# Layer 2 of a four-layer kernel: the third tile is fetched one step earlier, and the second step's order is rewritten

## The chip, the cores and the metric

The kernel runs on one core of one Trainium2 chip. The metric is the device time of one execution in microseconds (us), given as the median of three runs. All stages run one after the other in one launch, so a microsecond saved anywhere on the path is a microsecond of the total.

## The reference

Four layers work on the same array `x` of 32 x 64 x 512 floats, 2048 rows of 512. Each adds a feed-forward part to `x`: an attention and mixture-of-experts block (layer 0), a mixture of 32 experts (layer 1), a soft mixture of experts behind a low-rank adapter (layer 2), and an attention over cached blocks with an int8 product (layer 3). The change lies in layer 2:

```python
H = einsum('btd,od->bto', x, W)
delta = einsum('btr,bor->bto', einsum('btd,brd->btr', x, A[idx]), Bm[idx]) * s[idx]
y = H + delta                                  # the adapter product
x_ln = layernorm(y); x_n = l2norm(x_ln)
logits = einsum('bnd,des->bnes', x_n, mu_n)    # 16 experts x 128 slots = 2048 slots
dispatch = softmax(logits, over the 64 rows n of one batch entry)
combine = softmax(logits, over the 2048 slots of one row)
h = gelu(einsum('besd,edh->besh', einsum('bnd,bnes->besd', x_ln, dispatch), W1) + b1)
out = einsum('bsd,bns->bnd', h @ W2 + b2, combine)
x = x + out
```

## The kernel before

**Tiles and steps.** The 2048 rows are 16 tiles of 128 rows (two batch entries each). `layer2` has a loop over `i` from 0 to 16, here called step 0, step 1 and so on. Step `i` computes the logits and both softmaxes of tile `i` (class `Softmaxes`), mixes tile `i-1` (class `Mix`), and forms the adapter product and norm of tile `i+1` (class `Lora` and `l2_norm_pieces`). Tiles 0 and 1 are fetched and put through the adapter ahead of the loop.

**Pieces of a step.** `logits(q)` (L1396, four quarters of 512 slots) writes `lp`; VectorE scales it into `lT` (L1401) and keeps a running maximum `mx` (L1409 to L1413). `over_rows(q)` is the first softmax (`eT`: L1421, L1422, the Exp at L1425), and `divide(q)` divides by its sums (`inv` on VectorE at L1432 and L1433, the product on GpSimd at L1434). `highest()` transposes `mx` (PE L1440), takes the row maximum (`mr`, L1442) and spreads it on a diagonal (`dg`, L1444). `over_slots()` multiplies that diagonal by ones (`bp`, PE L1450), subtracts it from the four `lT` (VectorE L1452) and takes their Exp (ScalarE L1453). `hidden(q)` is the product with W1 (`zp`, PE L1473; `z`, VectorE L1475). `turn(q)` transposes weights (`ep` L1482, copied to `ew` L1484), `sums()` adds the slots' weights (`csum` L1492, `csb` L1497), `dispatch(q)` is the product `hp` (L1505) with its Gelu (`h`, L1510), `total()` is the product `dp` (L1515) with its reciprocal `rd`, `combine(q)` the product `gp` (L1528) with its copy `gT`, `project(q)` the product `out` (L1539). `Lora.turn`, `.adapter` and `.product` are the PE products `tp` (L1320, copied to `fT` on ScalarE at L1322), `ap` (L1329, masked into `am` at L1333) and `yp` (L1341, L1342). `l2_norm_pieces` begins with the statistics `st`, `mv`, `ve` (L1360 to L1364).

**Fetching a tile.** `combined.fetch` loads a tile's rows (`xt`), gathers four rows of expert outputs for each row (`yk`, GpSimd's queue, L284), and hands back four additions (VectorE L1025) which the step places by hand. Before the change tile 2 is fetched in step 1, tile 3 in step 2, and so on.

**`hidden` moves between steps.** In step 0 there is nothing to mix, so step 0 computes `hidden` of tile 0 itself. Step 1 therefore has no `hidden` pieces. From step 2 on, each step computes the four `hidden` pieces of the tile that it mixes, and puts them beside `highest` and `over_slots`.

**Order.** [...] `g.pin` and `g.first` fix instructions in the order in which the program writes them. `cache_rows` is a side job: each `next(rows)` gathers 112 rows on GpSimd's queue (`kvst`, one buffer) and writes them back by SP's queue (`oldkv`). It lies in the same GpSimd queue as the gathers of `fetch` and the products of `divide`. PSUM has two buffers under the tag `tp`, which `tp`, `ap`, `bp`, `ep` and `dp` share, and two under `mm`, which `lp`, `zp`, `csum` and `yp` share.

Of the kernel before, what the change touches and what calls it, by code (L numbers as in the profile page):

```python
# [22 lines left out]
NT = B * T // P  # L23
# [1155 lines left out]
def layer2(g, w, combined, first, w3):  # L1179
    tc, nc, a = g.tc, g.nc, g.a  # L1180
    with ExitStack() as ctx:
        pool = lambda name, bufs, **kw: ctx.enter_context(
            tc.tile_pool(name=name, bufs=bufs, reuse_waits="tile", **kw)
        )
        wp = pool("l2w", 1)
        sb = pool("l2sb", 1)
        s2 = pool("l2s2", 2)
        ps = pool("l2ps", 2, space=PSUM)
        xs, xb = g.stream("x2"), g.stream("x2b")
        x = [combined(sb, 0, 3), combined(sb, 1, 3)]  # L1190
        for k in ("gamma", "beta"):
            w[k] = g.load_bcast(wp, k)
        yp = [Lora(g, w, sb, s2, ps, x[i], i).run() for i in range(2)]
        xn = l2_norm(g, w, sb, s2, yp[0])
        w["b1"] = g.load_bcast(wp, "b1", eng=nc.scalar, later=True)
        for k in ("w2", "b2"):
            w[k] = g.load(wp, k, nc.scalar, True)
        w["bias3"] = g.load_bcast(wp, "bias3", eng=nc.scalar, later=True)
        xnT, nn = g.transpose4(ps, s2, xn[0], "xnT2"), xn[1]
        xn = l2_norm(g, w, sb, s2, yp[1])  # L1200


        last = None
        rows = cache_rows(g, sb, w3)
        for i in range(NT + 1):
            soft = Softmaxes(g, w, sb, s2, ps, xnT) if i < NT else None
            mix = Mix(g, w, sb, s2, ps, x[i - 1], *last) if last else None
            adds = []
            if last and i + 1 < NT:
                t, adds = combined.fetch(sb, i + 1, 3)  # L1210
                x.append(t)
            if mix and not soft:
                mix.turn(0)
                mix.turn(1)
            if soft:
                for q in range(4):
                    soft.logits(q)
                    if mix and q < 2:
                        mix.turn(q)
                    soft.over_rows(q)  # L1220
                    if q % 2 == 0:
                        next(rows, None)
                    if q > 0:
                        soft.divide(q - 1)
            if i == 0:
                z = Mix(g, w, sb, s2, ps, None, None, None, xnT, nn, None)
            else:
                z = mix if mix.z is None else None
            if z:
                z.hidden(0)  # L1230
            if soft:
                soft.divide(3)
            for add in adds[0:2]:
                add()
            if z:
                z.hidden(1)
                next(rows, None)
            if soft:
                soft.highest()
            for add in adds[2:4]:  # L1240
                add()
            if z:
                z.hidden(2)
            if soft:
                soft.over_slots()
            if z:
                z.hidden(3)
                next(rows, None)
            if mix:
                lora = Lora(g, w, sb, s2, ps, x[i + 1], i + 1) if i + 1 < NT else None  # L1250
                if lora:
                    lora.turn()
                mix.sums()
                mix.dispatch(0)
                if lora:
                    lora.adapter()
                mix.turn(2)
                if lora:
                    norm = l2_norm_pieces(g, w, sb, s2, lora.product())
                    next(norm)  # L1260
                    if i + 2 == NT:

                        w3["w_kv3"] = first.tile([P, 4, D], F32, name="w_kv3", tag="sb_w_2")
                        g.dma(w3["w_kv3"], a["w_kv3"])
                        w3["x3"] = [first.tile([P, D], F32, name="x3", tag=f"sb_{k}") for k in ("w_a", "w_b")]
                        for j in range(2):
                            g.dma(w3["x3"][j], xs[j * P : (j + 1) * P, :])
                mix.total()
                mix.combine(0)
                mix.dispatch(1)  # L1270
                mix.turn(3)
                if lora:
                    next(norm)
                mix.project(0)
                next(rows, None)
                mix.combine(1)
                if lora:
                    xn = next(norm)
                mix.dispatch(2)
                mix.project(1)  # L1280
                mix.combine(2)
                mix.dispatch(3)
                mix.project(2)
                next(rows, None)
                mix.combine(3)
            before = xnT, nn
            if i + 1 < NT:
                xnT, nn = g.transpose4(ps, s2, xn[0], "xnT2", pin=True), xn[1]
            if mix:
                mix.bias()  # L1290
                mix.project(3)
                mix.finish(xs, xb, i - 1)
            last = (soft.eT, soft.lT, *before, z.z if i == 0 else None) if soft else None
        for _ in rows:
            pass
        return xs, xb


def cache_rows(g, sb, w3):

    w3["rows"] = g.dram.tile([B, 3, CH, D], F32, name="oldkv")
    for b in range(B):
        for c in range(3):
            t = sb.tile([CH, D], F32, name="kvst", bufs=1)
            g.gather(t, g.a["kv"], w3["gidx"][0:CH, c * B + b : c * B + b + 1], later=True)
            g.dma(w3["rows"][b, c], t)
            yield
# [43 lines left out]
def l2_norm(g, w, sb, s2, yp):  # L1351

    *_, out = l2_norm_pieces(g, w, sb, s2, yp)
    return out


def l2_norm_pieces(g, w, sb, s2, yp):
    nc = g.nc
    st = s2.tile([P, 6], F32, name="st")
    g.pin(nc.vector.bn_stats(st, yp))  # L1360
    mv = s2.tile([P, 2], F32, name="mv")
    nc.vector.bn_aggr(mv, st)
    ve = s2.tile([P, 1], F32, name="ve")
    g.pin(nc.vector.tensor_scalar(ve, mv[:, 1:2], 1e-5, None, ALU.add))  # L1364
    rs = g.power(s2, ve, "nhalf", "rs")
    yield
    xl = sb.tile([P, D], F32, name="xl")
    g.pin(nc.vector.tensor_scalar(xl, yp, mv[:, 0:1], rs, ALU.subtract, ALU.mult))
    nc.gpsimd.tensor_tensor(xl, xl, w["gamma"], ALU.mult)
    nc.gpsimd.tensor_tensor(xl, xl, w["beta"], ALU.add)  # L1370
    sq = sb.tile([P, D], F32, name="sq2", tag="mx")
    ss = s2.tile([P, 1], F32, name="ss2")
    nc.scalar.activation(sq, xl, AF.Square, accum_out=ss)
    nn = g.power(s2, ss, "half", "nn")
    yield
    g.pin(nc.vector.tensor_scalar(nn, nn, 1e-12, None, ALU.max))  # L1376
    rn = s2.tile([P, 1], F32, name="rn")
    nc.vector.reciprocal(rn, nn)
    g.pin(nc.vector.tensor_scalar(xl, xl, rn, None, ALU.mult))
    yield xl, nn  # L1380
# [749 lines left out]
def program(tc, a):  # L2130
    with ExitStack() as ctx:
        g = Prog(tc, a, ctx)
        w3 = {}
        pool3 = ctx.enter_context(tc.tile_pool(name="w3", bufs=1))
        bridge, combined = layer0(g, w3, pool3)
        first = ctx.enter_context(tc.tile_pool(name="w2a", bufs=1, reuse_waits="tile"))
        with tc.tile_pool(name="w2", bufs=1, reuse_waits="tile") as pool:
            w2 = {"pool": pool}
            beside = layer2_ahead(g, first, pool, w2)
            combined = layer1(g, bridge, combined, beside, w2)  # L2140
            for _ in beside:
                pass
            xs, xb = layer2(g, w2, combined, first, w3)
        layer3(g, w3, xs, xb)
# [17 lines left out]
```

## Time and profile before

| | us |
|---|---|
| median of 3 runs (lowest, highest) | 2708.14 (2706.84, 2720.64) |
| the profiled execution | 2699.47 |
| its span | 2697.7 |
| step 0 of layer 2 (first `lp` product to the next step's first) | 1259.95 to 1292.43: 32.5 |
| step 1 | 1292.43 to 1353.86: 61.4 |
| step 2 | 1353.86 to 1417.86: 64.0 |

The span is the time between the first and the last recorded instruction; 1.8 us of the execution lie outside it. In a timeline the first column is the start in us from the span's beginning and the second the duration; brackets at the end give the engine's idle time before the instruction and what ended it. In a table by stretches, "(x)" counts instructions, and PEclk is the share of TensorE's full clock that was granted in the stretch.

### The profile page before, as it was taken

To read this page: it belongs to the slowest core of one execution; us is meant where nothing else is said; L and a number is where in the kernel's file an instruction comes from. 1 tells how busy PE (TensorE), PEld (TensorE's weight loads), DVE (VectorE), ACT (ScalarE), POOL (GpSimd) and SP (SyncE) were. 2 spreads that over 40 slices of the span, in tenths; PEclk is the share of its full clock that TensorE was granted. 3 is DMA by queue.
4 is the path that set the end of the run, shared out by engine and by line. 5 is a ranking of instruction groups with operands and counts; after the bars stand their busy time and mean duration, and the time that the engine had idled before them with its cause. 6 is when DMAs were issued, how large, how long until landed. Compare 5 with 4: busy or idle time off the path is not lost.

```text
span 2697.7 us, 42340 instructions
## 1 busy us (share of the span) xinstructions
PE 2526.4 (94%) x16523; PEld 1623.4 (60%) x16523; DVE 1416.6 (53%) x3439; ACT 723.6 (27%) x1501; POOL 850.8 (32%) x904
## 2 busy tenths in 40 slices
PE   6999998996699999996899999999999999989998
PEld 5777775563565555564566666666666665435554
DVE  4666655643744444444444444555554431557886
ACT  2344430111311121010222222222222221236664
POOL 2222214623232233212222333233332321563440
PEclk9999999997699999997899999999999999999999
DMA  2333214445656976544222222222222222523441
GB/s 98 131 123 116 90 70 169 158 151 196 214 181 226 339 260 227 201 163 169 59 69 69 73 81 82 74 73 72 73 73 76 80 71 99 182 77 108 136 138 48
DMA packets 136213, 343.58 MB, mean 127 GB/s; under 512 B 24249, under 2 KB 25049, under 8 KB 128704
## 3 DMA queue, kind: packets, MB, share of 16 engines
q1 hardware_dynamic: 100368, 245.84, 26.4%
q0 software_dynamic: 35056, 89.13, 11.0%
q10 hardware_dynamic: 576, 5.77, 0.5%
q8 instruction: 134, 2.20, 0.3%
q14 instruction: 79, 0.65, 0.1%
HBM read 247.10 MB, written 109.58 MB: 132 GB/s over the span
## 4 chain that ended last, share of the span: by engine, by line
PE 43%; DVE 8%; issue 1%; DMA 1%; ACT 0%; POOL 0%; another core or an unknown queue 0%; SPq 0%; ACTq 0%; POOLq 0%; DVEq 0%
PE out L1539 8%; PE lp L1396 7%; PE pp L1852 3%; PE gp L1528 3%; PE zp L1473 3%; PE y L2099 2%; PE yp L1341 2%; PE op L2077 2%; PE pT L2052 2%; PE hp L1505 2%; PE sp L2030 2%; DVE xt L1025 1%; PE ep L1482 1%; DVE inv L1432 1%; PE kp L2003 1%
## 5 line engine op out<-in xcount | busy, mean ns | idle before, releaser
L943 PE MATMUL gu<-xT,wt 128*128 128x320 f32 x1472 | 407.8, 433 | 0.0
L943 PEld LDWEIGHTS gu<-xT,wt 128*128 128x128 f32 x1472 | 278.2, 191 | 123.1 <-issue 16.2
L1539 PE MATMUL out<-sb_w,gT 128*128 128x512 f32 x512 | 233.6, 599 | 11.1 <-DVE nn L1376 6.7
L1396 PEld LDWEIGHTS lp<-xnT,sb_mu 128*128 128x128 f32 x2048 | 236.1, 194 | 8.7 <-issue 6.7
L962 PE MATMUL y<-wt,hT 128*128 128x512 f32 (+1 forms) x552 | 239.4, 605 | 1.2 <-DVE yo L971 0.7
L1396 PE MATMUL lp<-xnT,sb_mu 128*128 128x128 f32 x2048 | 239.1, 277 | 1.5 <-DVE xnT L256 0.8
L1473 PE MATMUL zp<-sb_w,xnT 128*128 128x512 f32 x512 | 228.3, 595 | 2.7 <-DVE z L1475 2.6
L284 POOL DMA_INDIRECT kvst<-kv,gidx x96 | 96.8, 1009 | 264.4 <-DMA oldkv<-kvst 190.3
L1532 DVE COPY gT<-gp 128x512 f32<-128x512 f32 x64 | 44.3, 691 | 248.4 <-PE gp L1528 248.0
L1539 PEld LDWEIGHTS out<-sb_w,gT 128*128 128x128 f32 x512 | 93.4, 190 | 116.2 <-issue 95.2
L1473 PEld LDWEIGHTS zp<-sb_w,xnT 128*128 128x128 f32 x512 | 93.7, 190 | 110.5 <-issue 97.4
L284 POOL DMA_INDIRECT xr<-rows,stok x115 | 110.1, 957 | 150.2 <-PE tp L924 79.7
L962 PEld LDWEIGHTS y<-wt,hT 128*128 128x128 f32 (+1 forms) x552 | 80.3, 171 | 99.7 <-issue 83.1
L284 POOL DMA_INDIRECT kvt<-newkv,oidx x96 | 98.0, 1021 | 131.9 <-DMA kvt<-oldkv 99.1
L677 POOL TENSOR_TENSOR ga<-ga,sg 128x320 f32<-128x320 f32 x64 | 55.2, 862 | 265.5 <-ACT sg L673 265.5
L284 POOL DMA_INDIRECT yk<-ys,slot x96 | 97.6, 1016 | 126.3 <-SPq L823 65.3
L1510 ACT ACTIVATE h<-hp 128x512 f32<-128x512 f32 x128 | 69.5, 594 | 222.2 <-PE hp L1505 222.1
L673 ACT ACTIVATE sg<-ga 128x320 f32<-128x320 f32 x64 | 30.0, 469 | 277.1 <-DVE ga L671 271.1
L924 PEld LDWEIGHTS tp<-sb_cst,xr 128*128 128x128 f32 x460 | 53.5, 146 | 66.0 <-issue 40.1
L971 DVE TENSOR_TENSOR yo<-y,bd 128x512 f32<-128x512 f32 (+1 forms) x96 | 66.3, 690 | 50.8 <-PE y L962 47.2
L1434 POOL TENSOR_TENSOR eT<-eT,inv 128x512 f32<-128x512 f32 x64 | 71.9, 1125 | 64.9 <-DVE inv L1433 59.5
L1401 DVE TENSOR_TENSOR lT<-lp,cmu 128x512 f32<-128x512 f32 x64 | 43.5, 680 | 92.3 <-PE lp L1396 86.2
(379 smaller groups left out, 4558.1 us busy)
## 6 DMA issues: line engine op xcount, KB each, us to landing
wt<-w_e SPq DMA_DIRECT2D x32, 1538.0 KB
ys<-yo SPq DMA_DIRECT2D x115, 256.0 KB
oldkv<-kvst SPq DMA_DIRECT2D x96, 224.0 KB
kvt<-oldkv SPq DMA_DIRECT2D x96, 224.0 KB
ys<-zero SPq DMA_DIRECT2D x10, 2048.0 KB
xt<-x SPq DMA_DIRECT2D x62, 256.0 KB
x<-xt SPq DMA_DIRECT2D x48, 256.0 KB
wt<-w_e SPq DMA_DIRECT2D x7, 1536.0 KB
```

Source lines behind the costliest of these rows:

```text
L284: ins = self.nc.gpsimd.indirect_dma_start(out=out, out_offset=None, in_=src, in_offset=bass.IndirectOffsetOnAxis(ap=idx, axis=0), **kw)
L677: nc.gpsimd.tensor_tensor(ga, ga, sg, ALU.mult)
L943: nc.tensor.matmul(o, wj[:, c, ic * P : (ic + 1) * P], xT[:, c, :], start=c == 0, stop=c == 3)
L962: nc.tensor.matmul(y[row : row + n, :], hTs[u][:, ic, col : col + n], wd[:, ic, :], start=ic == 0, stop=ic == 1,)
L971: nc.vector.tensor_tensor(yo[r], y[r], bd[r], ALU.add)
L1396: g.first(e + c, nc.tensor.matmul(lp[:, e, :], w["mu"][:, c, (4 * q + e) * P : (4 * q + e + 1) * P], self.xnT[:, c, :], start=c == 0, stop ...
L1434: g.pin(nc.gpsimd.tensor_tensor(e3, e3, inv.unsqueeze(2).to_broadcast([P, 8, T]), ALU.mult))
L1473: g.first(c, nc.tensor.matmul(zp, self.xnT[:, c, :], w["w1"][:, c, cols], start=c == 0, stop=c == 3))
L1510: g.pin(nc.scalar.activation(self.hs[q][b], hp[:, b], AF.Gelu))
L1528: g.first(e + b + k, nc.tensor.matmul(gp[r, e, cols], self.hs[q][b][:, e, r], self.lT[q][:, e, cols], start=True, stop=True))
L1539: g.first(e, nc.tensor.matmul(self.out, self.gTs[q][:, e, :], w["w2"][:, 4 * q + e, :], start=q + e == 0, stop=q + e == 6 and q == 3))
L1852: nc.tensor.matmul(pp, xT[i][:, c, :], (w["w_kv3"] if z else wq)[:, c, :], start=c == 0, stop=c == 3)
```

## The change

Tile 2 is fetched in step 0 instead of step 1: its row load, its four gathers and its four additions are placed beside the `hidden` pieces of tile 0. Steps from 2 on fetch as before.

In the step that has a softmax and a mix and no `hidden` pieces (only step 1), the order is written anew. After the logits it was: `divide(3)`, two additions, `highest`, two additions, `over_slots`, then `lora.turn`, `sums`, `dispatch(0)`, `lora.adapter`, `mix.turn(2)`, `lora.product` with the norm's first piece, `total`, `combine(0)`, `dispatch(1)`. It becomes: `lora.turn`, `sums`, `lora.adapter`, `highest`, `divide(3)`, `dispatch(0)`, `lora.product` with the norm's first piece, `over_slots`, `mix.turn(2)`, `total`, `combine(0)`, `dispatch(1)`. What follows is as before. No arithmetic is added or removed. On ScalarE, `dispatch(0)`'s Gelu now comes ahead of `over_slots`'s Exp, so that step 1 has two activation-table loads more.

```diff
@@ -1206,8 +1206,8 @@
             soft = Softmaxes(g, w, sb, s2, ps, xnT) if i < NT else None
             mix = Mix(g, w, sb, s2, ps, x[i - 1], *last) if last else None
             adds = []
-            if last and i + 1 < NT:
-                t, adds = combined.fetch(sb, i + 1, 3)
+            if len(x) < NT and i != 1:
+                t, adds = combined.fetch(sb, max(i + 1, 2), 3)
                 x.append(t)
             if mix and not soft:
                 mix.turn(0)
@@ -1226,28 +1226,45 @@
                 z = Mix(g, w, sb, s2, ps, None, None, None, xnT, nn, None)
             else:
                 z = mix if mix.z is None else None
-            if z:
-                z.hidden(0)
-            if soft:
+
+            early = soft and mix and not z
+            lora = Lora(g, w, sb, s2, ps, x[i + 1], i + 1) if mix and i + 1 < NT else None
+            if early:
+                lora.turn()
+                mix.sums()
+                lora.adapter()
+                soft.highest()
                 soft.divide(3)
-            for add in adds[0:2]:
-                add()
-            if z:
-                z.hidden(1)
-                next(rows, None)
-            if soft:
-                soft.highest()
-            for add in adds[2:4]:
-                add()
-            if z:
-                z.hidden(2)
-            if soft:
+                mix.dispatch(0)
+                norm = l2_norm_pieces(g, w, sb, s2, lora.product())
+                next(norm)
                 soft.over_slots()
-            if z:
-                z.hidden(3)
-                next(rows, None)
-            if mix:
-                lora = Lora(g, w, sb, s2, ps, x[i + 1], i + 1) if i + 1 < NT else None
+                mix.turn(2)
+                mix.total()
+                mix.combine(0)
+                mix.dispatch(1)
+            else:
+                if z:
+                    z.hidden(0)
+                if soft:
+                    soft.divide(3)
+                for add in adds[0:2]:
+                    add()
+                if z:
+                    z.hidden(1)
+                    next(rows, None)
+                if soft:
+                    soft.highest()
+                for add in adds[2:4]:
+                    add()
+                if z:
+                    z.hidden(2)
+                if soft:
+                    soft.over_slots()
+                if z:
+                    z.hidden(3)
+                    next(rows, None)
+            if mix and not early:
                 if lora:
                     lora.turn()
                 mix.sums()
@@ -1268,6 +1285,7 @@
                 mix.total()
                 mix.combine(0)
                 mix.dispatch(1)
+            if mix:
                 mix.turn(3)
                 if lora:
                     next(norm)
```

Built, the instruction order of each engine differs from before in these places alone: PE in step 1; VectorE in steps 0 and 1 (the four additions go from step 1 to step 0); ScalarE in step 1 (with the two table loads); GpSimd's queue, where the four `yk` gathers now stand ahead of the first `kvst` gather of step 0 and not behind the fourth. SP's queue is unchanged: the row load of tile 2 already stood ahead of the loop.

## The prediction

> **What bounds the kernel now.** I read the page's busy shares and its clock row first, then the busy time by stretches for steps 0 to 3 of layer 2, then the timelines of PE and VectorE in step 1.
>
> ```profile
> PE 2526.4 (94%) x16523; PEld 1623.4 (60%) x16523; DVE 1416.6 (53%) x3439; ACT 723.6 (27%) x1501; POOL 850.8 (32%) x904
> ...
> PEclk9999999997699999997899999999999999999999
> ```
>
> PE is busy 94% of the span, so time is to be had only where PE stands still or runs slow. The clock row has two dips; the second is at 1215 to 1349 us (slices 19 and 20), where layer 2 begins.
>
> ```profile
> 1292.40:1353.90 61.50, 51.83 (x434) 37.92 (x435) 27.42 (x50) 13.83 (x24) 15.87 (x16) 0.89 0.19 56
> 1353.90:1417.90 64.00, 62.12 (x467) 41.14 (x466) 30.72 (x54) 15.76 (x26) 20.23 (x20) 1.00 0.24 73
> ```
>
> Columns: stretch, length, busy time of PE, PEld, DVE, ACT, POOL, then clock, DMA share, GB/s. Step 1 (first line) has 16 `zp` products' worth less PE work than step 2 (4 pieces of 3.43 us = 13.7) yet is only 2.6 us shorter: PE idles 9.7 us in it and gets 0.89 of its clock. The timeline of PE says where:
>
> ```profile
> 1300.55 7.31 PE L1396 MATMUL lp<-xnT,sb_mu 128*128 128x128 f32 x64
> 1310.56 0.45 PE L1440 MATMUL tp<-sb_cst,mx 128*128 128x128 f32 x1 [2.70 <-DVE mx L1413]
> 1316.44 0.77 PE L1450 MATMUL bp<-dg,sb_cst 128*128 128x128 f32 x2 [5.44 <-DVE dg L1444]
> 1317.80 1.11 PE L1320 MATMUL tp<-sb_cst,xt 128*128 128x128 f32 x4 [0.59 <-DVE xt L1025]
> 1318.85 1.94 PE L1492 MATMUL csum<-lT,sb_cst 128*32 128x128 f32 x32
> 1320.71 2.08 PE L1505 MATMUL hp<-z,ew 64*128 64x128 f32 x16
> ...
> 1384.93 1.08 PE L1492 MATMUL csum<-lT,sb_cst 128*32 128x128 f32 x32
> 1385.94 1.16 PE L1505 MATMUL hp<-z,ew 64*128 64x128 f32 x16
> ```
>
> After the last logits (1307.86) PE waits 2.70 for the maximum, 5.44 for `dg`, 0.59 for tile 2's sum: 8.73 us. Then `csum` and `hp` take 1.94 and 2.08 where step 2 (last two lines) takes 1.08 and 1.16: half clock. On VectorE:
>
> ```profile
> 1310.12 0.29 DVE L1413 TENSOR_TENSOR mx<-mx 128x128 f32<-128x128 f32 x1
> ...
> 1313.40 2.38 DVE L1025 SCALAR_TENSOR_TENSOR xt<-yk,gates,xt 128x512 f32<-128x512 f32 x2
> ...
> 1316.01 0.29 DVE L1444 TENSOR_SCALAR dg<-sb_cst,mr 128x128 f32<-128x128 f32 x1
> ```
>
> `dg` stands behind tile 2's first two additions, which is most of the 5.44. The granted clock was 0.50 from 1310.1 to 1323.7.
>
> [...]
>
> ```profile
> 1306.70:1310.10 3.40, 1.16 (x11) 0.96 (x9) 3.28 (x6) 0.63 (x1) 1.04 (x1) 1.00 0.37 110
> 2211.20:2214.60 3.40, 1.92 (x36) 1.57 (x34) 0.17 (x1) 2.85 (x4) 0.51 (x1) 1.00 0.25 67
> 1037.00:1040.40 3.40, 1.96 (x12) 1.05 (x12) 2.08 (x4) 0.59 (x1) 2.58 (x3) 1.00 0.56 151
> ```
>
> The first two windows (PE busy 1.16 and 1.92 us) were followed by half clock, the third (1.96) was not[...]. [...] The trace has the 1.28 (at 1358.67)[...]. [...] two additions took 2.38 while GpSimd worked on `eT`, 1.53 (1316.21) while it did not.
>
> **The change, part by part.**
>
> *Step 1, PE.* New order from 1307.86, start to start as in step 2 at full clock: `tp` 0.53, `csum` 1.01, `ap` 0.99, `tp` of `mx` 0.27, `hp` 1.10, `yp` 3.43 and 0.86, `bp` 0.30, `ep` 0.44: 8.93, so `dp` could start at 1316.8. The first three (2.53) fill the wait for `mx`, which ends at 1310.41. `fT` gets its ScalarE slot between two Exps, about 1308.5 to 1309.1, and `csum` covers it. VectorE, free from 1312.57, does `csb`, `am`, `mr`, `dg` (0.29, 0.29, 0.28, 0.29) by about 1313.7; `yp` covers that to 1316.05. Both old waits go.
>
> *What is late next.* `dp` takes the `tp` buffer of `bp`, which is free only after the four subtractions of L1452. These now stand behind the norm's statistics, which wait for `yp`: `yp` done 1316.2, `st` to `ve` 1.02 (1329.12 to 1330.14 before), four subtractions 2.47: 1319.7. So `dp` starts at 1319.75, not 1316.8: **a new PE wait of 2.95 us.** Queued behind it are `gp`, `hp`, `ep`, `out`. Before, `dp` started at 1328.92. Gain 9.2.
>
> *Clock again.* [...] I take 2.2 (bounds 0 and 3.2).
>
> *Two table loads*, 1.28 each. The Exp load falls at 1314.9 to 1316.2, ahead of the first subtraction's end (1317.9); the second Gelu load ends about 1322.2, when `hp` of `dispatch(1)` ends, and its Gelus (1.09) are done about 3 us before `gp` of `combine(1)` asks for them, behind 3.43 of `out`. Cost 0[...].
>
> *Step 0, VectorE.* Two additions (2.2 beside `eT`, as at 1377.15 in step 2) go ahead of `z1`, two (1.5) ahead of `z2`.
>
> ```profile
> 1284.15 0.75 DVE L1475 SCALAR_TENSOR_TENSOR z<-zp,nn,bc_b 128x512 f32<-128x512 f32 x1 [0.28 <-PE zp L1473]
> ...
> 1289.08 2.42 ACT L1453 ACTIVATE lT<-lT 128x512 f32<-128x512 f32 x4 [6.83 <-DVE lT L1452]
> 1291.79 0.59 ACT L254 COPY xnT<-tp 128x512 f32<-128x512 f32 x1 [0.29 <-PE tp L295]
> ```
>
> `dg` moves from 1285.4 to 1287.2, still ahead of `bp` at 1287.49. The subtractions start at 1289.2, not 1288.37; the four Exps end 3.13 later (as before), at 1292.3, and the copy `xnT`, behind them on ScalarE, starts there and not at 1291.79. PE's next logits wait for it: cost 0.5 (bounds 0 and 2).
>
> *Step 0, GpSimd's queue and DMA.* Four gathers at 1266.7 (1.25 apart) put `kvst` back to 1271.8. The second `kvst` waits for its write-back, 6.3 us from gather to gather at rest (1285.21 to 1291.45), 10.2 while the 4 MB of `w2` arrive (1266.67 to 1276.89): 1278 to 1282 for 1276.89. Behind it stands `eT` of q 1, whose end `inv` of q 3 needs (two `inv` buffers) at 1282.96; it would end at 1280 to 1284. At the near end it is hidden, at the far end it costs 1 to 2, in the bound above. The gathers' data have until 1283.9; from issue to sum took 3.7 at 1239.32 and 7.2 for the `kvst` under load. SP's order does not change; tile 2's row load was issued by 1228.5.
>
> *Sum.* 9.2 - 2.2 - 0.5 = **6.5 us** less: 2693.0 for the profiled execution of 2699.47. That one lay 8.7 below the median of the runs; against the median, 2708.14 - 6.5 = **2701.6**.
>
> **Rivals.**
> - *PE stays warm* in the new wait[...]. Gain 8.7: 2699.4.
> - *Step 0 pays more*: `kvst` returns at 1283 or later, `eT`, `inv` and the additions slip behind it, and PE waits 2 to 4 us more. For: the weights' load is under way. Against: it fades by 1272 (344 GB/s in 1270 to 1272, 27 in the next 2 us). Gain about 3: 2705.
> - *It does not show*: gain under 2, 2706 to 2709, if both happen.
> - *Slower*: `yk` lands late in step 0. VectorE stands at the first addition with `z1`, `mr` and `dg` behind it, and PE at `bp`, 1 us for 1 us. It cancels the gain if the data come 6 to 7 us after 1283.9, some 24 us after the first issue; at 34 us the kernel is 10 us slower, 2718. Nothing in the trace lands that late.
>
> **How the numbers follow.** Half clock after the new wait 0.55; warm 0.2; step 0 pays more 0.14; no effect 0.08; slower 0.03. The runs shown differ by 14 us, so the median itself may move by some 5 us. Range: 2699.4 less 6, to 2708 with 3 more: 2693 to 2711. What a measurement here can tell from no change is about 0.5%, 13.5 us. Step 1 exceeds step 2 less its `zp` pieces by 61.4 - (64.0 - 13.7) = 11.1 us, and no edit here can gain more. Faster by over 0.5% needs the runs' scatter besides: 0.08. Within: 0.89. Slower by over 0.5%: 0.03.
>
> **What would show it.** Step 1 at 54 to 55 us; `tp` of L1320 right after the logits with no wait; `bp` without a wait on `dg`; a wait of about 3 us before `dp` (L1515), released by VectorE's `lT`; half clock for 3.4 to 6.8 us after it; step 0 longer by 0.5 to 1, with `xnT` behind four Exps. I am wrong if `dp` waits under 2 us, if PE waits for `z` or `bp` in step 0 for over 2 us, or if steps from 2 on change.

## The result and the profile after

The changed kernel took 2704.84 us (median of 13 runs, 2696.22 to 2710.53) against 2710.99 for the kernel before on the same chip (13 runs). The ratio is 0.9971 with a 95% interval of 0.9961 to 0.9982: 7.9 us less, between 5 and 11 (the two medians differ by 6.2). Run again beside the experiments, it gave 0.9974 (0.9961 to 0.9986). The prediction was 6.5 us less. The gain is real and lies within the half per cent that the prediction took as the least that can be told from no change; with 13 runs of each kernel the measurement was finer than that.

The profiled execution took 2703.36, with a span of 2701.6, which is *longer* than the 2697.7 of the execution profiled before. The stages tell why: up to layer 2 it lay 5.3 us behind the other (1243.7 us against 1238.4), in layer 2 it gained 6.4 (1035.5 against 1041.9), and after layer 2 it lost 4.8 (422.3 against 417.5), in stages whose code is the same in both. Over all the profiled executions of this study the start of layer 2 lies between 1237.7 and 1246.3 us. Layer 2 scatters too: steps 2 to 14, whose code is the same in every kernel here, took 826.0 us before and 829.3 after. A change of a few us is therefore read inside its own steps, and the total from many runs.

The busy time by stretches, for steps 1 and 2 after (columns as before: stretch, length, PE, PEld, DVE, ACT, POOL, clock, DMA share, GB/s):

```profile
1297.90:1351.10 53.20, 49.99 (x433) 36.85 (x434) 23.96 (x46) 16.59 (x26) 12.57 (x13) 0.97 0.15 45
1351.10:1414.70 63.60, 62.08 (x467) 41.17 (x466) 30.74 (x54) 15.77 (x26) 20.36 (x20) 1.00 0.24 73
```

Step 1 takes 53.2 us, not 61.4; PE idles 3.2 in it, not 9.7, and its mean clock is 0.97, not 0.89. The timeline of PE in step 1 after the last logits:

```profile
1306.05 7.31 PE L1414 MATMUL lp<-xnT,sb_mu 128*128 128x128 f32 x64
1313.19 0.60 PE L1338 MATMUL tp<-sb_cst,xt 128*128 128x128 f32 x4
1313.72 1.08 PE L1510 MATMUL csum<-lT,sb_cst 128*32 128x128 f32 x32
1314.73 1.16 PE L1347 MATMUL ap<-fT,sb_w_a 128*128 128x128 f32 x8
1316.06 0.30 PE L1458 MATMUL tp<-sb_cst,mx 128*128 128x128 f32 x1 [0.17 <-DVE mx L1431]
...
1321.78 0.38 PE L1468 MATMUL bp<-dg,sb_cst 128*128 128x128 f32 x2
1322.00 0.60 PE L1500 MATMUL ep<-sb_cst,eT 128*128 128x128 f32 x4
1325.62 0.35 PE L1533 MATMUL dp<-sb_cst,csb 128*128 128x1 f32 x2 [3.02 <-DVE lT L1470]
...
1327.18 2.08 PE L1523 MATMUL hp<-z,ew 64*128 64x128 f32 x16
...
1351.11 3.73 PE L1414 MATMUL lp<-xnT,sb_mu 128*128 128x128 f32 x32
```

(Lines past the loop's start are 18 higher than before.) The adapter's transposes, `csum` and `ap` run at full clock (1.00 granted from 1297.9 to 1326.6) in the time in which PE used to wait for the maximum; the maximum costs 0.17, `bp` no wait at all. Then comes the new wait, 3.02 us before `dp`, ended by VectorE's `lT`, and `hp` behind it runs at half speed (2.08 for 1.16). VectorE shows what `dp` waited for:

```profile
1321.98 0.70 DVE L1378 BATCH_NORM_STATS2 st<-yp 128x6 f32<-128x512 f32 x1 [1.78 <-PE yp L1360]
...
1323.00 2.47 DVE L1470 TENSOR_TENSOR lT<-lT,bp 128x512 f32<-128x512 f32 x4
```

The subtractions end at 1325.47, and `dp`, which takes over `bp`'s buffer, starts at 1325.62. The half clock that follows lasts 3.4 us in this execution and 6.8 in the second profile of the same kernel (first fence the first profile, second fence the other; the clock is the third number from the end):

```profile
1326.70:1330.10 3.40, 3.40 (x33) 3.06 (x29) 1.41 (x2) 2.00 (x3) 1.27 (x1) 0.50 0.02 5
```

```profile
1325.20:1332.00 6.80, 5.82 (x55) 5.33 (x56) 2.41 (x5) 4.55 (x8) 1.74 (x2) 0.50 0.01 2
```

ScalarE's two further table loads are hidden, as its timeline shows:

```profile
1320.38 1.28 ACT L1471 ACT_TABLE_LOAD   x1
1323.71 2.42 ACT L1471 ACTIVATE lT<-lT 128x512 f32<-128x512 f32 x4 [2.05 <-DVE lT L1470]
...
1326.63 1.28 ACT L1528 ACT_TABLE_LOAD   x1
1329.31 1.08 ACT L1528 ACTIVATE h<-hp 128x512 f32<-128x512 f32 x2 [1.40 <-PE hp L1523]
```

After each load ScalarE still waits, 2.05 us for VectorE and 1.40 for PE.

Step 0 pays on PE in two places:

```profile
1292.29 0.49 PE L1468 MATMUL bp<-dg,sb_cst 128*128 128x128 f32 x2 [0.21 <-DVE dg L1462]
...
1297.93 3.84 PE L1414 MATMUL lp<-xnT,sb_mu 128*128 128x128 f32 x32 [1.27 <-ACT xnT L254]
```

The wait for `xnT` was 0.68 before, and `bp` had none. From the first `zp` of step 0 to step 1's first `lp` it is 16.43 us against 15.35, 1.1 longer.

### The profile page after: what moved, and what is told of

Its sections match the earlier page's. It is cut to its first block, busy times and chain, and to the rows that moved or that the text cites. A ratio compares the mean times of both kernels' runs of the same rounds, so it can differ in the third digit from the quotient of the medians.

```text
span 2701.6 us, 42326 instructions
## 1 busy us (share of the span) xinstructions
PE 2524.0 (93%) x16508; PEld 1620.7 (60%) x16523; DVE 1417.6 (52%) x3439; ACT 725.6 (27%) x1503; POOL 852.3 (32%) x904
## 4 chain that ended last, share of the span: by engine, by line
PE 41%; DVE 9%; issue 2%; DMA 1%; ACT 1%; POOL 0%; another core or an unknown queue 0%; SPq 0%; ACTq 0%; POOLq 0%; DVEq 0%
PE out L1557 8%; PE lp L1414 7%; PE pp L1870 3%; PE gp L1546 3%; PE zp L1491 3%; PE yp L1359 2%; PE y L2117 2%; PE hp L1523 2%; PE op L2095 2%; PE pT L2070 2%; PE sp L2048 2%; DVE xt L1025 1%; PE ep L1500 1%; DVE inv L1450 1%; PE kp L2021 1%
## 5 line engine op out<-in xcount | busy, mean ns | idle before, releaser
L2055 DVE CUSTOM_DVE_ANT_0 s<-sp,mask 128x336 f32<-128x336 f32 x128 | 60.8, 503 | 59.8 <-PE sp L2048 25.1
```

What stands on the lines that cost most here:

```text
L2055: nc.vector.tensor_tensor_reduce(p, sps[j], self.masks[2 * i + half], -0.0625, 3.0e38, ALU.add, ALU.min, m)
```

## The experiments

My theory (A): PE work put into the two waits gives the gain; the new wait before `dp` with the half clock behind it takes part of it back, and the additions take a little in step 0. The rivals: the gain is only that of the additions leaving `dg`'s path; or (theory C) the new wait or the half clock costs next to nothing, since other work hides it.

**Each part alone.** First the early fetch with step 1 in its old order:

```diff
-            early = soft and mix and not z
+            early = False
```

> The early fetch alone, with step 1 in its old order (less the four additions). Theory A (the gain comes from PE work put into the waits): only the additions leave the path of dg; dg can end about 1.5 us after the last division's sums, so the wait before bp falls from 5.44 to about 3.2 us and the 0.59 before L1320 goes, while the wait for the maximum (2.7) and the half clock after it stay. Step 1: 58 to 59 us (before 61.4, with the whole change 53.2), the kernel 2 to 3 us faster than before. Rival B (the additions ahead of dg were what cost, the new order adds little): step 1 at 53 to 55 us, the kernel 6 to 8 us faster.

Measured: step 1 at 58.1 us; ratio to the kernel before 0.9978 (0.9966 to 0.9990). The timeline of PE in step 1:

```profile
1316.01 0.45 PE L1458 MATMUL tp<-sb_cst,mx 128*128 128x128 f32 x1 [2.71 <-DVE mx L1431]
1319.55 0.77 PE L1468 MATMUL bp<-dg,sb_cst 128*128 128x128 f32 x2 [3.10 <-DVE dg L1462]
```

`bp` waits 3.10 instead of 5.44, the maximum 2.71 as ever. Step 1 is where theory A put it, 3.3 us shorter than before. The whole time points the same way; its interval (3 to 9 us) reaches above the 2 to 3 that I wrote and does not separate the theories by itself.

Then the new order with tile 2 fetched in step 1 as before:

```diff
-            if len(x) < NT and i != 1:
-                t, adds = combined.fetch(sb, max(i + 1, 2), 3)
+            if last and i + 1 < NT:
+                t, adds = combined.fetch(sb, i + 1, 3)
...
             if early:
+                for add in adds:
+                    add()
                 lora.turn()
```

> The new order of step 1 alone; tile 2 is fetched in step 1 as before, and its four additions stand just ahead of the transposes L1320. Theory A: all of step 1's rearranged PE work waits behind the additions, which VectorE reaches only after the last quarter's softmax (about 12.6 us into PE's old idle time's start plus 3.9 us for four additions), so PE idles about 8.7 us in one piece, runs at half clock after it, and then has the new wait before dp as well: step 1 at 62 to 66 us, the kernel 0 to 5 us slower than before. Rival B (the order alone does it): step 1 under 58 us.

Measured: step 1 at 63.8 us; ratio 1.0009 (0.9996 to 1.0022).

```profile
1316.01 1.09 PE L1340 MATMUL tp<-sb_cst,xt 128*128 128x128 f32 x4 [8.51 <-DVE xt L1025]
...
1330.01 0.35 PE L1535 MATMUL dp<-sb_cst,csb 128*128 128x1 f32 x2 [3.02 <-DVE lT L1472]
```

One wait of 8.51 us for the additions in place of three, half clock after it (`csum` 1.94 for 1.08, `ap` 1.75 for 1.16), and the wait before `dp` on top: 2.3 us longer than before. So within step 1 the order without the early fetch is worth less than nothing (in the whole time its interval includes no change), and the fetch without the order 3.3 us. Together they give 7.1 to 8.3: the additions must be done for PE to have work to put into the wait.

**The new wait.** `bp` and the subtractions go between the fourth and the fifth product of `yp`, ahead of the norm's statistics, and `dp` goes behind the next `gp` and `hp`. `Lora.product` is split for this into `most`, the first four products, and `rest`, the fifth; that part of the edit is left out here:

```diff
-                norm = l2_norm_pieces(g, w, sb, s2, lora.product())
-                next(norm)
-                soft.over_slots()
-                mix.turn(2)
-                mix.total()
-                mix.combine(0)
-                mix.dispatch(1)
+                most = lora.most()
+                soft.over_slots()
+                norm = l2_norm_pieces(g, w, sb, s2, lora.rest(most))
+                next(norm)
+                mix.turn(2)
+                mix.combine(0)
+                mix.dispatch(1)
+                mix.total()
```

> The changed kernel with the wait before dp taken out: bp and the four subtractions come between the fourth and the fifth yp product, ahead of the norm's statistics, and dp comes behind gp and hp of the next pieces. Theory A: the 3.02 us of PE idle before dp go to under 0.5, and with them the half clock after it[...]: step 1 at 48.5 to 50 us against 53.2, the kernel some 4 us faster than the changed one. Rival B (the next stage waits for VectorE or for the Gelu instead: gT, whose copy stands behind the subtractions, or h): PE waits 2 to 3 us before out or gp, step 1 at 52 to 53.

Measured: step 1 at 49.2 us; ratio to the kernel before 0.9952 (0.9932 to 0.9972), 13 us. The timeline of PE, and the whole of step 1 by its stretch (PE's clock is the third number from the end):

```profile
1316.19 0.38 PE L1476 MATMUL bp<-dg,sb_cst 128*128 128x128 f32 x2
1316.41 1.02 PE L1368 MATMUL yp<-sb_w_b,am 128*128 128x512 f32 x2
...
1317.80 1.15 PE L1554 MATMUL gp<-lT,h 128*64 128x64 f32 x32
...
1320.92 0.63 PE L1508 MATMUL ep<-sb_cst,eT 128*128 128x128 f32 x4 [0.56 <-DVE rd L1543]
```

```profile
1293.20:1342.40 49.20, 48.44 (x434) 35.40 (x435) 23.89 (x46) 16.57 (x26) 12.56 (x13) 1.00 0.17 48
```

The wait is gone but for 0.56 us, the clock stays full (1.00 over the step), and nothing takes the wait's place at `out` or `gp`. Against the changed kernel's 53.2 and 54.3 us (two profiles), 4.0 to 5.1 us had been left there. The edit moves two things, the reads of `bp` forward and `dp` back; neither was tried alone.

**The half clock by itself.** PE's idle time before `dp` is filled with products that nobody reads, six in one run and three in the other:

```diff
                 mix.turn(2)
+                spare = ps.tile([P, D], F32, name="spare", tag="acc", bufs=1)
+                for _ in range(6):
+                    g.pin(g.nc.tensor.matmul(spare, lora.xT[:, 0, :], w["w_2"][:, 0, :], start=True, stop=True))
                 mix.total()
```

> The changed kernel with six extra products of 128 x 512 (fT by w_2, into a PSUM bank that nobody reads at that time) put between ep and dp of step 1: 2.6 us of PE work that replaces idle time, nothing else. Theory A (half clock after the wait costs time of its own): dp starts when it did, PE's idle before it falls from 3.02 to about 0.5 us, no half clock follows, and the time from dp's start to step 2's first lp falls from 25.5 (26.8 in the run with late additions) to about 24.1 us; step 1 at 51.5 to 52 us. Rival B (the half clock is hidden behind VectorE's and ScalarE's work): dp to lp stays at 25.5, step 1 at 53.2.

Measured: six products came to 12 records and 5.32 us, not 2.6, so they pushed `dp` back by 2 us; step 1 took 54.7. From `dp` to step 2's first `lp` it took 25.08 us, and the ratio was 0.9983 (0.9973 to 0.9993). My working had counted half of PE's work: 2.6 us is what three products take. With `dp` pushed back, the run answers only in part. With three:

> As the filled kernel, with three extra products instead of six: a product of 128 x 512 in float32[...] (12 records of 0.43 us were seen for six products), so three fill 2.6 us of the wait and dp is no longer pushed back. Theory A (a full clock after the wait saves all of the half-speed time): from dp's start to step 2's first lp 24.1 us against 25.5[...] and 26.6 to 26.8[...]. Theory C (at full clock PE comes upon the waits for nn and gT that stood at this place before the change, 0.9 to 1.05 us together, so the half clock costs only the rest): 24.9 to 25.1 us. In both, dp starts 3.6 us after ep and no half clock follows it.

Measured: step 1 at 53.0 us, in a single execution, so that only its steps are read and not its whole time. PE:

```profile
1324.86 2.74 PE L1245 MATMUL spare<-sb_w,fT 128*128 128x512 f32 x6
1328.05 0.35 PE L1536 MATMUL dp<-sb_cst,csb 128*128 128x1 f32 x2 [0.44 <-DVE lT L1473]
...
1337.34 3.70 PE L1560 MATMUL out<-sb_w,gT 128*128 128x512 f32 x8 [0.57 <-DVE nn L1397]
...
1343.82 3.70 PE L1560 MATMUL out<-sb_w,gT 128*128 128x512 f32 x8 [0.61 <-DVE gT L1553]
```

No half clock here: `gp` and `hp` behind `dp` took 1.15 and 1.16 us, and from `dp` to `lp` it took 25.27. The other profiles with these two as quick took 24.94 (before), 24.96 (early fetch alone) and 25.08 us (six fillers). The changed kernel took 25.49 us with 3.4 us at half clock and 26.60 with 6.8. The run below took 26.77, with `gp`, `hp` and `ep` slow (1.97, 2.08 and 1.11), and the new order alone 25.83, with `gp` and `hp` slow (1.93 each). So 25.27 lies above both forecasts, nearest to theory C: at full clock PE comes upon the old waits for `nn` and `gT`, 1.18 us here, of which it meets none or 0.25 in the four profiles with slow products. Measured against 25.27, the half clock costs 0.2 to 0.6 us net where fewer products are slow and 1.3 to 1.5 where more are; half of the 3.4 and 6.8 us, my estimate of what is lost at half speed, would be 1.7 and 3.4.

**The additions in step 0.** They are moved behind the last `z`, into VectorE's idle time before step 1:

```diff
+                held, adds = (adds, []) if i == 0 else ([], adds)
                 for add in adds[0:2]:
...
                     z.hidden(3)
                     next(rows, None)
+                for add in held:
+                    add()
```

> The changed kernel with the four additions of step 0 moved behind the last z of step 0. Theory A: the additions ahead of z1 and z2 cost step 0 about 1 us by way of dg (wait before bp 0.21) and of the Exps ahead of xnT (wait 1.27 against 0.68); they go, and the additions fit into VectorE's idle time before step 1's first lT (4.4 us): the time from the first zp of step 0 to step 1's first lp falls from 16.43 to 15.4 us, step 1 stays at 53.2. Rival B (step 0 is bound by PE anyway): no change, 16.4. By the clock, 1 us is within the uncertainty of the whole time.

Measured: first `zp` to step 1's `lp` 15.75 us; step 1 at 54.5, with `gp`, `hp` and `ep` behind `dp` at 1.97, 2.08 and 1.11 us for 1.15, 1.16 and 0.66; ratio 0.9960 (0.9944 to 0.9976). `lp` waits for `xnT` 0.68 us as before the change. Of the 0.4 us that is left above 15.35, most is the third `zp`, which starts 0.3 later behind a late `z`. How much the additions themselves cost is seen best between runs that are otherwise alike in step 0. This run and the second profile of the changed kernel (below) share a late first `z` on VectorE: 15.75 against 16.66. The next run and the first profile share quick logits ahead of `zp` (15.94 us in both): 15.35 against 16.43. With the wait before `dp` gone as well:

> The kernel without the wait before dp, and with the additions of step 0 behind the last z: both edits together. Theory A (they sit in different steps and add up): step 1 at 49.2 us as without the wait, first zp of step 0 to step 1's first lp at 15.4 to 15.8 us (15.71 without the wait, 16.43 with the whole change), the kernel 0 to 1 us faster than without the wait alone and 11 to 13 us faster than before. Rival B (the additions now collide with step 1's first lT or with the transposes of tile 2): step 1 over 49.8.

Measured: 15.35 us and step 1 at 49.2; ratio 0.9952 (0.9939 to 0.9966). In the steps the two edits add up. In the whole time this version cannot be told from the one without the wait alone: the ratios are the same. Both are clearly faster than the kernel before. The changed kernel, on the same chip as this version, had a median of 2703.4 us against 2698.7 here and a ratio of 0.9974; the intervals overlap, so that the lead over it is clear in the steps and only likely in the total.

> The changed kernel once more. [...]step 1 takes 53.2 or 54.5 us; the wait itself stays at 3.0 us. Step 0's wait of lp for xnT stays between 1.0 and 1.3 us.

Measured: step 1 at 54.3 us with 6.8 us at half clock, the wait before `dp` again 3.02; from `zp` to `lp` 16.66. VectorE in step 0 of this run, and GpSimd at the same time:

```profile
1285.05 2.20 DVE L1440 TENSOR_TENSOR eT<-lT,m 128x512 f32<-128x512 f32 x1
```

```profile
1284.66 0.95 POOL L284 DMA_INDIRECT kvst<-kv,gidx  x1 [5.01 <-DMA oldkv<-kvst]
1285.63 1.06 POOL L1452 TENSOR_TENSOR eT<-eT,inv 128x512 f32<-128x512 f32 x1
```

The subtraction of `eT` took 2.20 us instead of 0.69 while GpSimd's product of `eT` ran; by the records it began 0.58 us ahead of that product and ended 0.56 us after it. In the run with three fillers, whose step 0 is the same code, the subtraction took 0.69, and step 0 paid nothing at all (15.35 us); the early fetch alone and the six fillers paid nothing either. My reading is that the cost in the second profile comes from where GpSimd's product lands; it starts behind the second `kvst`, which came 8.0 and 8.2 us after the first in the two profiles of the changed kernel. It was not tested by an edit of GpSimd's queue. It is not the only way to pay: in the first profile of the changed kernel the subtraction took 0.69 too, and the next section has the reason.

## Why the prediction was right, point by point

- *Filling step 1's waits: right.* From the start of the last two `lp` quarters to `dp` it took 28.37 us before (1300.55 to 1328.92), 19.20 was forecast (to 1319.75), and 19.57 came (1306.05 to 1325.62): a gain of 8.8 at `dp` for 9.2. Of the missing 0.4, 0.17 is the wait left at the `tp` of `mx`, and 0.11 lies in `yp`, whose eight records took 3.54 us start to start for 3.43.
- *The new wait before `dp`: right*, 3.02 us for 2.95, with the buffer and the releaser named.
- *Half clock after it: right that it comes, the term was mis-sized.* I subtracted 2.2 us, my estimate, which no trace had shown. In the terms of that sum it is what was added between `dp` and step 2's first `lp`, which took 24.94 us before, 25.49 and 26.60 after: 0.55 with 3.4 us at half clock and 1.66 with 6.8. I counted the lost half-speed time in full, but part of it lies over waits that PE meets at full clock (0.50 and 0.42 us below). PE before the change, at a granted clock of 1.00:

```profile
1328.92 0.28 PE L1515 MATMUL dp<-sb_cst,csb 128*128 128x1 f32 x2
...
1338.07 3.70 PE L1539 MATMUL out<-sb_w,gT 128*128 128x512 f32 x8 [0.50 <-DVE nn L1376]
...
1344.36 3.70 PE L1539 MATMUL out<-sb_w,gT 128*128 128x512 f32 x8 [0.42 <-DVE gT L1532]
...
1353.86 3.73 PE L1396 MATMUL lp<-xnT,sb_mu 128*128 128x128 f32 x32
```

- *What makes the clock fall: not settled.* That half clock would follow the new wait was my estimate. It did, in all four profiles that had the 3.02 us. But how much PE work in a stretch of 3.40 us keeps the clock up was not shown: beside the prediction's 1.92 us, followed by half clock, and 1.96, not followed by it, the trace before has a stretch with 2.36 us of work that was followed by half clock, and one with 1.84 that was not:

```profile
398.74:402.14 3.40, 2.36 (x19) 2.15 (x20) 1.10 (x4) 0.21 (x1) 0.00 (x0) 1.00 0.41 154
402.15:405.55 3.40, 3.40 (x18) 3.40 (x18) 1.71 (x14) 0.00 (x0) 0.00 (x0) 0.50 0.00 0
...
2412.60:2416.00 3.40, 1.84 (x13) 0.96 (x11) 0.08 (x1) 0.00 (x0) 2.59 (x3) 1.00 0.25 65
2416.00:2419.40 3.40, 0.00 (x0) 0.00 (x0) 0.04 (x1) 0.00 (x0) 3.00 (x3) 1.00 0.21 57
```

- *Two table loads at nothing: right*: 1.28 us each, with 1.40 us to spare at the nearer one.
- *Step 0: mis-sized the other way.* 0.5 forecast, 1.1 and 1.3 in the two profiles of the changed kernel, within the bounds of 0 and 2. The step that failed is VectorE's timetable: I moved `z1` and `dg` by the additions alone. In fact the first `z` itself came 5.94 and 6.18 us after the first `zp`, not 5.26 as before. In the second profile that is the slow subtraction shown above. In the first it is PE that was early: its half clock at the start of the logits lasted 3.4 us there and 6.8 before, so that the four quarters took 15.94 us for 17.30 before. VectorE reached `z` 21.7 us after the first `lp`, much as in the run with three fillers, in which step 0 paid nothing (21.8), and so stood behind a PE that was over 1 us ahead. `dg` ended 10.74 and 10.98 us after the first `zp`, where the forecast comes to 10.1.
- *The sum: 6.5 us.* First `zp` of step 0 to step 2's first `lp` took 76.78 us before, 69.61 and 70.96 in the two profiles after: 7.2 and 5.8 less (8.8 less 0.55 and 1.1, and 8.8 less 1.66 and 1.3). The two mis-sized terms nearly cancel, so that the close agreement of the sum is in part luck.
- *The bound of 11.1 us: wrong.* The prediction says that no edit can gain more in step 1. Taking the new wait out brought step 1 from 61.4 to 49.2, 12.2 less. Step 2, from which the bound was worked out, has 1.9 us of PE idle time of its own.
- *The profiled execution: wrong.* 2693.0 was forecast from the one before, 2703.36 came: 10 us of scatter in stages that the change does not touch.
- *Steps from 2 on, whose change was to be a sign of being wrong.* Steps 2 to 14 took 826.0 us before, 829.3 and 828.8 in the two profiles after. The change does not seem to be the reason: with the same code in these steps, four profiles on one chip took 825.7 to 826.9 and three on another, the second of the changed kernel among them, 828.8 to 829.7. On which chips the profile before and the first one after were taken is not on record, so that this stays open.
- *Rivals.* The clock stayed up in none of the four profiles that had the whole wait (the changed kernel twice, the new order alone, the additions moved): `hp` behind it took 1.93 to 2.08 us for 1.16. The gathers landed in time (the first addition in step 0 followed `inv` without a wait), so the slower case did not arise.

## What to carry to other kernels

Independent PE work put into a wait pays only when its inputs are ready ahead of that wait: here each half of the edit alone gave 3.3 us or less than nothing in step 1, and both gave 7 to 8. After such a move, ask at once which instruction takes over the moved one's PSUM buffer, and whose reads free it: the 3 us before `dp` came from there, and moving the reads ahead of the norm's statistics, with `dp` placed later, gave them back. When a step of a few us is judged, compare the step in the traces, since other stages of the same execution differ by more than the change.

## What the runs showed of the hardware that was not expected

- After the same 3.02 us of idle the granted clock was 0.50 for 3.4 us in one profile of the changed kernel and for 6.8 in the other, and only 0.2 and 1.3 us of it reached the end of the step.
- A product of 128 x 512 in float32 shows as two matmul records of about 0.43 us each: three products filled 2.74 us of PE time, six 5.32.
- VectorE's subtraction of `eT` stretched from 0.69 to 2.20 us beside one GpSimd product of 1.06 us: it lost more than that product's own length. It ended 0.56 us after the product, though its record begins first.
